# A graph-network kernel whose instruction order is written by a planner: another buffer rule, a transfer model, byte masks and other planning parameters

## The chip, the cores and the metric

The kernel runs on one core of one Trainium2 chip. Its time is the device time of one execution in microseconds (us). A core has five engines, each executing its own queue in order: TensorE (PE, matmuls and transposes), VectorE (DVE), ScalarE (ACT), GpSimd (POOL) and SyncE (SP, which here only issues transfers). They wait for each other through semaphores. Tiles lie in SBUF, 128 partitions wide; matmul results lie in PSUM, in eight banks. Everything is fp32 unless said otherwise.

## The reference

There are 32 samples of 512 nodes with 256 features. Four graph layers run in sequence; each one's result is added to its input x, which has been layer-normalised (and passed through relu) ahead of the layer. Cut to what matters:

```python
for layer in (L0, L1, L2, L3):
    x = x + layer(relu(layernorm(x)), adj)

def L0(x):                     # 4-head attention, heads of 64
    s = where(adj == 0, -inf, q @ k.T / 8)
    return softmax(s) @ v @ wo.T + bo
def gat(x, W, a, mask):        # graph attention
    h = x @ W
    e = leaky_relu(h @ a[:F] [:, None] + h @ a[F:] [None, :], 0.2)
    return elu(softmax(where(mask, e, -9e15)) @ h)
def L1(x):                     # two GATs with MLPs, the first without a mask
    o = relu(x @ mlp1_w + b1);  o = elu(gat(o, W_fc, a_fc, all)) + o
    o = relu(o @ mlp2_w + b2);  return relu(elu(gat(o, W_hand, a_hand, adj)) + o)
def L2(x): ...                 # 4-head GAT, heads of 64, masked by adj > 0
def L3(x): ...                 # 8-head GAT, heads of 32, logits plus beta * log(adj), then @ W_out
```

So every sample has eighteen 512x512 attention matrices in fp32, and no sample depends on another.

## The kernel before

**One sample.** A 512x512 matrix is kept transposed, as four tiles of 128 nodes by 512 (`p0`, `p1`, `p2`, `p3`). A tile of 128x512 f32 is called a block. All blocks come from one SBUF tag, `block`, with `BLOCKS` = 60 buffers; matmul results come from the eight PSUM banks. x is a tile of 128x4x256 with five buffers, loaded by SP, updated in place by the four layers and stored by SP; the load for a sample can start when the output of the sample five before it has left.

- `norm_t` makes statistics (DVE `stats`, `mv`), `rs` on POOL, `h` on ACT, transposes to `pt` on PE and `hT` on ACT.
- `layer0`: `qT`, `kT`, `v0`, scores `sc` on PE, exp on ACT, product with `mask0T` on DVE, additions into `total` on DVE, then `av` and the column sums `sm` on PE. `normalise` sends the sums through DRAM (`s1`, `few`, reciprocal, `s2`, `rc`) to get them on all partitions, and DVE makes `oT`; wo multiplies it. The bias is added to x by an accumulating transfer issued by POOL (`x<-boa`).
- `layer1`: mlp1 (`o1`), `first_gat` with `W_fc` (matmuls of 258 and 256 columns; row sums through the transposes of `total` and of `rs1`), mlp2 (`o3`), `second_gat` with `W_hand` (`v2`, `p2`, products with `mask1T`).
- `layer2` and `layer3` share `separable`: ACT's exp of a row broadcast `R` (eight or four transfers from DRAM by SP), then one DVE instruction for maximum and product with the mask (`mask1T`, `mask3T`). The sums over the tiles (`total`) are added by DVE for the first four heads and by accumulating transfers, issued by POOL (`p<-p`), for the last four.

**The order.** The layers do not issue instructions; they record them as `Step`s in a `Plan` (L82). `Plan.add` finds the dependencies. `Plan.order` (L169) then takes steps one by one, always the one with the smallest `(start, due)`. The start comes from a model: the engine's time, the operands' times by `cost()` (L333), release times of the samples (`STARTS`, `PACE`, `LAYERS`), and buffers. `due` comes from `PERIOD` times the sample, the length of the chain behind the step, and an offset `URGENT` for its tile's name and layer, a table of some hundred numbers. Up to four samples beyond the oldest are interleaved (`AHEAD`).

For a new tile the planner takes the buffer that comes free first by its model; it keeps some in reserve (`OWN`, `SPARE`, `KEEP`). `FILLED` = 10 blocks are withheld up to a modelled time of 190, because the preparation of masks and weights uses them:

```python
free["block"][:FILLED] = [FILLED_TO] * FILLED
...
when = max(when, sorted(free[tag])[n])
...
free[tag].remove(min(free[tag]))
```

A transfer has a length that depends on its size only, whatever else is under way. `Plan.issue` (L281) emits the steps in the order found; each engine then executes in this order, waiting where an operand or a buffer is not there. Since a helper records every step, all instructions of the four layers stand under one line in the profile, L297, and are told apart by the tiles' names.

Of the kernel before, what the change touches and what calls it, by code (L numbers as in the profile page):

```python
# [12 lines left out]
F32 = mybir.dt.float32  # L13
BF16 = mybir.dt.bfloat16
I32 = mybir.dt.int32
AF = mybir.ActivationFunctionType
# [4 lines left out]
P = 128  # L21
N = 512
NT = N // P
D = 256
# [9 lines left out]
H3, F3 = 8, 32  # L34
# [9 lines left out]

PERIOD = 107.0
STARTS, PACE = (0.0, 4.0, 19.0, 123.0), 101.0
LAYERS = (0.0, 32.0, 34.0, 184.0)

URGENT = {
    "stats:0": -231, "mv:0": -37, "rs:0": -123, "ms:0": -205, "h:0": 11, "pt:0": -750, "hT:0": 14, "mm:0": -216,  # L50
    "sc:0": -122, "p0:0": -65, "total:0": -98, "av:0": 34, "sums:0": -578, "s1:0": 49, "few:0": -6, "s2:0": 16,
    "rc:0": -235, "oT:0": 85, "mv:1": -1, "rs:1": -312, "ms:1": 79, "h:1": -294, "pt:1": -8, "hT:1": 210, "o1:1": 230,
    "sd:1": -3, "v1:1": 496, "nd:1": -243, "ew:1": 150, "p1:1": 192, "total:1": -170, "sm:1": 80, "rs1:1": -271,
    "rc:1": 295, "av:1": -43, "y:1": -155, "e:1": -181, "o2:1": 223, "o3:1": 97, "v2:1": -74, "sd2:1": 230,
    "mn:1": -599, "None:1": 532, "ew2:1": 73, "p2:1": 326, "rs2:1": -12, "u:1": 67, "x:1": 261, "stats:2": 253,
    "mv:2": -2, "ve:2": -111, "rs:2": 9, "ms:2": 327, "h:2": -217, "pt:2": 246, "hT:2": -176, "mm:2": -27,
    "vs:2": -140, "es4:2": -547, "e4:2": 121, "rd:2": -46, "R:2": 10, "p3:2": -509, "av:2": -104, "total:2": -557,
    "sm:2": 273, "r4:2": -73, "ue:2": -350, "x:2": -11, "stats:3": -7, "mv:3": -124, "ve:3": 186, "rs:3": 271,
    "ms:3": -493, "pt:3": 488, "hT:3": -507, "mm:3": -191, "vs:3": -282, "es8:3": 187, "e8:3": -10, "rT:3": -676,
    "rd:3": 450, "R:3": 367, "p3:3": -733, "av:3": -428, "total:3": 545, "sm:3": -50, "sums:3": 213, "raw:3": 11,  # L60
    "s1:3": 84, "s2:3": 121, "rc:3": -208, "oT:3": 42, "None:3": 359, "af:3": 10, "top:3": 409, "ok:3": 38,
    "values:3": -217, "rows:3": 208, "gp:3": -60, "gram:3": -190, "gab:3": 123, "sq:3": -31, "tp:3": -40,
    "res:3": 224,
}
BLOCKS, KEEP = 60, 2
KEEP_BANKS = 0
# [15 lines left out]
class Plan:  # L82
# [11 lines left out]
    OWN = dict(block=8, bank=2)  # L94
    SPARE = dict(block=2, bank=1)

    SWITCH = dict(full=0.094, columns=0.12, rows=0.2)
# [26 lines left out]
    def add(self, attribute, engine, op, args, kw):  # L124
# [8 lines left out]
        step.urgent = URGENT.get(f"{self.kinds.get(out.tensor.name)}:{step.layer}", 0.0)  # L133
        step.lasts = step.busy + lasts
        writes = [out] + ([kw["accum_out"]] if "accum_out" in kw else [])
        reads = [v for v in list(args) + list(kw.values()) if isinstance(v, bass.AP) and not any(v is w for w in writes)]
        for ap, writing in [(v, False) for v in reads] + [(v, True) for v in writes]:
            if ap.tensor.name not in self.tile_tag:
                continue
            name, box = ap.tensor.name, extent(ap)  # L140
            if name not in step.touches:
                step.touches.append(name)
            record = self.history.setdefault(name, [])
            for other, obox, owriting in record:
                bank = writing and owriting and step.engine == other.engine == "PE"
                if (writing or owriting) and other is not step and (bank or overlap(box, obox)):
                    if other not in step.before:
                        step.before.append(other)
                        other.after.append(step)
            record.append((step, box, writing))  # L150
# [6 lines left out]
    def behind(self, ap):  # L157

        self.gate = [step for step, _, writing in self.history[ap.tensor.name] if writing]

# [8 lines left out]
    def order(self):  # L169
# [16 lines left out]
        free = {tag: [0.0] * bufs for tag, (bufs, _) in self.tags.items()}  # L186
        free["block"][:FILLED] = [FILLED_TO] * FILLED
        held = {}
# [9 lines left out]
        for steps in self.samples:  # L198
            for step in steps:
                if not step.waits:  # L200
                    open_[step.engine].append(step)
        result, count, mode = [], sum(map(len, self.samples)), "full"
        oldest = 0

        def slots(step):

            when, taken = 0.0, {}
            for name in step.touches:
# [15 lines left out]
                if len(free[tag]) - n <= reserve:  # L224
                    return None
                when = max(when, sorted(free[tag])[n])
                taken[tag] = n + 1
            return when

        while len(result) < count:  # L230
            best = None
            for engine, waiting in open_.items():
                for step in waiting:
# [3 lines left out]
                    if engine == "PE" and step.mode != mode:  # L237
                        start = max(start, at[engine] + self.SWITCH[mode])
                    if best is not None and self.key(start, step) >= best[0]:
                        continue  # L240
# [7 lines left out]
            _, start, step = best  # L248
            step.start = start
            open_[step.engine].remove(step)  # L250
            at[step.engine] = start + step.busy
            if step.engine == "PE":
                mode = step.mode
            end = start + step.lasts
            for name in step.touches:
                tag, s = self.tile_tag[name], step.sample
                if name not in live:
                    live.add(name)
                    free[tag].remove(min(free[tag]))
                    held[s, tag] = held.get((s, tag), 0) + 1  # L260
                    to_come[s][tag] -= 1
                    pending[s, tag].remove(place[name])
                left[name] -= 1
                if not left[name]:
                    live.discard(name)
                    held[s, tag] -= 1
                    free[tag].append(end + self.HOP)
# [65 lines left out]
def cost(engine, op, args, kw, out):  # L333
# [15 lines left out]
    if engine == "DVE":  # L349
# [4 lines left out]
        by_pointer = op == "scalar_tensor_tensor" and isinstance(args[2], bass.AP)  # L354
        return 0.066 + 0.00105 * n + (0.06 if by_pointer else 0.0), 0.085
    if engine == "POOL":
        if op == "dma_start":
            return 1.1, (5.2 if n == N else 8.0)
        return (1.0 if n < 16 else 0.683), 0.1
    size = 4  # L360
    for _, k in (out.ap if out.tensor.name.startswith(("few", "R", "rc", "x")) else src.ap):
        size *= k
    return 0.4, 3.4 + size / 190e3


@with_exitstack
def gnn_stack_kernel(ctx: ExitStack, tc: tile.TileContext, a: dict, out: bass.AP):
# [59 lines left out]
    r3 = w3[:, :, 3 * H3 + D :]  # L427
    mask0T = const.tile([P, NT, N], BF16, name="mask0T")
    mask1T = const.tile([P, NT, N], BF16, name="mask1T")
    mask3T = const.tile([P, NT, N], F32, name="mask3T")  # L430
# [166 lines left out]
    def pipelined(stack):  # L597

        big = stack.enter_context(tc.tile_pool(name="big", bufs=1))
        psum = stack.enter_context(tc.tile_pool(name="psum", bufs=8, space=PSUM))  # L600
        dram = stack.enter_context(tc.tile_pool(name="dram", bufs=6, space=bass.MemoryType.DRAM))
        q = Plan(nc, PERIOD)
        def block(name):

            return q.tile(big, [P, N], name, BLOCKS, keep=KEEP, tag="block")

# [6 lines left out]
        def small(name, *free):  # L613
            return q.tile(big, [P, *free], name, 4)

        def half(b, t):
# [212 lines left out]
        def second_gat(o3, xt):  # L829

            v, sd = q.tile(big, [P, NT, D + 1], "v2", 2), small("sd2", NT, 2)
            for t in range(NT):
                ps = node_major(wh, t, o3, 0, D + 2)
                q.scalar.activation(v[:, t, :D], ps[:, :D], AF.Identity, bias=ones[:, 0:1])
                q.scalar.copy(sd[:, t, :], ps[:, D : D + 2])
            q.vector.memset(v[:, :, D : D + 1], 1.0)
            d = sd[:, :, 1]
# [12 lines left out]
            for t in range(0, NT, 2):  # L850
                e, u, avs, rs = block("e"), block("u"), [], small("rs2", 2, 2)
                for i in range(2):
                    av = bank("av")
                    avs.append(av)
                    for j in range(NT):
                        q.tensor.matmul(
                            av[:, : D + 1], p[j][:, col(t + i)], v[:, j, :], start=(j == 0), stop=(j == NT - 1)
                        )
# [33 lines left out]
        def separable(xt, w, nh, mask, bars):  # L892
# [12 lines left out]
            q.tensor.transpose(pt[: NT * nh, :P], es, ident)  # L905
            rT = q.tile(big, [P, P], "rT", 4, tag="turned")
            q.scalar.copy(rT[: NT * nh, :], pt[: NT * nh, :P])
            rd = q.tile(dram, [H3, N], "rd", 6)
            q.sync.dma_start(T(rd[:nh, :], "h (t p) -> t h p", p=P), rT[: NT * nh, :])
# [82 lines left out]
        def tests():  # L992
# [8 lines left out]
            for t in range(NT):  # L1001
                ai, af = q.tile(big, [P, N], "ai", BLOCKS, keep=KEEP, tag="block", dtype=I32), block("af")
                q.sync.dma_start(ai, a["adj"][t * P : (t + 1) * P, :])
# [55 lines left out]
        for i in range(B):  # L1059
# [11 lines left out]
        late = preparation(  # L1071
            lambda n: big.tile([P, N], F32, tag="block", name=n, bufs=BLOCKS),
            lambda n: psum.tile([P, N], F32, tag="bank", name=n, bufs=8),
# [424 lines left out]
```

## Time and profile before

| | before |
|---|---|
| median of 3 runs | 3901.18 us (3900.81 to 3904.83) |
| profiled execution, its own time | 3905.73 us |
| its span | 3903.9 us |
| mean granted TensorE clock | 0.995 |
| PE busy | 3824.9 us, 17400 matmuls and transposes |
| DVE busy | 3292.2 us, 7177 instructions |
| ACT busy | 2837.1 us, 6128 instructions |
| POOL busy | 519.1 us, 530 instructions |
| transfers | 292.65 MB, 1.6 thousand issues by SP and POOL in the loop over samples |

The profiled execution is 4.6 us above the median, and its span 1.8 us below its own time. A busy time is the sum of the durations that the profile gives; matmuls overlap by their pipelining, so PE's start-to-start distance is shorter than the mean of one. In the groups the DVE product with `mask3T` has a mean of 746 ns and occurs 1024 times, the DVE addition into `total` 686 ns and 808 times, ACT's exp of `R` 716 ns and 1536 times; an accumulating transfer of 256 KB lands 4.9 us after its issue.

### The profile page before, as it was taken

The numbers are of one execution on the slowest core, as the hardware profiler recorded it, in microseconds if no ns is written. First come the engines' busy times: TensorE is split into PE (matmuls) and PEld (weight loads), VectorE is DVE, ScalarE is ACT, GpSimd is POOL, SyncE is SP. The second block draws the span as 40 slices with busy tenths as digits, with TensorE's granted clock in tenths as the row PEclk, the third lists the DMA queues.
The fourth block names the chain that finished last, engine by engine and source line by source line (L and its number), as shares of the span: only waits on it lengthen the run. The fifth ranks groups of instructions, "written<-read, shape, count | busy, mean of one in ns | idle before, by whom it ended". The sixth has DMA issues, their size and how long they took to land.

```text
span 3903.9 us, 53766 instructions
## 1 busy us (share of the span) xinstructions
PE 3824.9 (98%) x17400; PEld 2230.5 (57%) x17400; DVE 3292.2 (84%) x7177; ACT 2837.1 (73%) x6128; POOL 519.1 (13%) x530
## 2 busy tenths in 40 slices
PE   8999999999999999999999999999999999999996
PEld 4555565555566555566565556565655555655643
DVE  5578988888988888988889988889888889888896
ACT  4567777777777767777677777677777777776784
POOL 0001110111110111110111111111101111101110
PEclk9999999999999999999999999999999999999998
DMA  3012331323332333332333323333323333314241
GB/s 100 19 48 61 88 93 52 92 61 82 88 84 59 93 61 82 87 76 67 82 63 89 89 66 78 81 63 88 93 58 85 70 73 88 88 55 94 46 110 48
DMA packets 217623, 292.65 MB, mean 75 GB/s; under 512 B 49915, under 2 KB 103422, under 8 KB 217334
## 3 DMA queue, kind: packets, MB, share of 16 engines
q0 software_dynamic: 68864, 111.18, 16.5%
q1 hardware_dynamic: 148196, 177.69, 14.6%
q8 instruction: 140, 2.29, 0.3%
q14 instruction: 149, 1.22, 0.1%
q10 hardware_dynamic: 274, 0.26, 0.0%
HBM read 158.79 MB, written 19.10 MB: 46 GB/s over the span
## 4 chain that ended last, share of the span: by engine, by line
PE 85%; ACT 8%; DVE 3%; issue 2%; DMA 2%; POOL 0%; SPq 0%; DVEq 0%; ACTq 0%; POOLq 0%
PE mm L297 43%; PE av L297 31%; PE pt L297 6%; ACT p L297 6%; PE sm L297 3%; DVE p L297 2%; PE sc L297 1%; DMA p<-p 1%; ACT h L297 1%; DVE total L297 1%; POOL rs L297 0%; DMA rc<-s 0%; DVE x L297 0%; DMA s<-few 0%; DVE rc L297 0%
## 5 line engine op out<-in xcount | busy, mean ns | idle before, releaser
L297 ACT ACTIVATE p<-R,e 128x512 f32<-128x512 f32 x1536 | 1001.5, 716 | 82.5 <-DVE total L297 75.6
L297 DVE SCALAR_TENSOR_TENSOR p<-p,e,mask3T 128x512 f32<-128x512 f32 x1024 | 715.0, 746 | 12.9 <-ACT p L297 12.9
L297 PE MATMUL av<-p,v 128*64 128x512 f32 (+1 forms) x2048 | 697.7, 597 | 6.6 <-ACT v L297 5.4
L297 DVE TENSOR_TENSOR total<-total,p 128x512 f32<-128x512 f32 x808 | 511.3, 686 | 0.1
L297 PE MATMUL av<-p,vs 128*32 128x512 f32 (+1 forms) x3072 | 497.9, 596 | 5.9 <-DVE p L297 5.9
L297 POOL TENSOR_TENSOR rs<-ve,mhalf 128x4 f32<-128x4 f32 x128 | 155.5, 1220 | 2367.8 <-DVE few L297 858.5
L297 POOL DMA_DIRECT2D p<-p x360 | 342.9, 1314 | 934.3 <-PE av L297 790.4
L297 PE MATMUL mm<-W_fc,o 128*128 128x256 f32 (+1 forms) x2048 | 459.5, 380 | 0.4 <-ACT o L297 0.4
L297 PEld LDWEIGHTS av<-p,v 128*64 128x64 f32 (+1 forms) x2048 | 257.6, 163 | 334.5 <-issue 278.1
L297 PEld LDWEIGHTS mm<-W_fc,o 128*128 128x128 f32 x2048 | 384.9, 190 | 83.3 <-issue 22.7
L297 DVE SCALAR_TENSOR_TENSOR p<-p,e,mask1T 128x512 f32<-128x512 f32 x512 | 352.8, 746 | 10.3 <-ACT p L297 10.1
L297 DVE TENSOR_TENSOR p<-p,mask0T 128x512 f32<-128x512 f32 x512 | 317.8, 686 | 13.9 <-ACT p L297 13.9
L297 ACT ACTIVATE h<-x,ms,rs 128x256 f32<-128x256 f32 x512 | 271.4, 593 | 69.9 <-DVE ms L297 69.8
L297 PEld LDWEIGHTS av<-p,vs 128*32 128x32 f32 (+1 forms) x3072 | 138.6, 119 | 310.0 <-issue 263.1
L297 DVE TENSOR_TENSOR total<-p,p 128x512 f32<-128x512 f32 x404 | 267.4, 690 | 39.0 <-PE av L297 22.6
L297 ACT ACTIVATE p<-sc 128x512 f32<-128x512 f32 x512 | 254.4, 673 | 3.7 <-PE sc L297 1.1
L297 PE MATMUL mm<-w,hT 128*128 128x272 f32 (+1 forms) x1024 | 253.5, 396 | 1.3 <-ACT hT L297 1.3
L297 PE MATMUL av<-v,p 128*128 128x257 f32 x1024 | 232.6, 380 | 2.7 <-ACT o L297 1.4
L297 PE MATMUL mm<-o,mlp_w 128*128 128x512 f32 x512 | 230.3, 593 | 2.1 <-DVE o L297 2.1
L297 PE MATMUL mm<-hT,mlp_w 128*128 128x512 f32 x512 | 230.9, 593 | 1.0 <-ACT hT L297 1.0
L297 PE MATMUL sc<-qT,kT 64*128 64x512 f32 x1024 | 228.9, 596 | 0.0
L297 ACT ACTIVATE e<-av,ones,rs 128x256 f32<-128x256 f32 x128 | 65.6, 562 | 220.8 <-PE av L297 108.6
(187 smaller groups left out, 5783.1 us busy)
## 6 DMA issues: line engine op xcount, KB each, us to landing
R<-rd SPq DMA_DIRECT2D x384, 256.0 KB
p<-p POOLq DMA_DIRECT2D x360, 256.0 KB, 4.9
x<-in_x_dram SPq DMA_DIRECT2D x32, 512.0 KB
x<-boa POOLq DMA_DIRECT2D x32, 512.0 KB, 6.5
rc<-s SPq DMA_DIRECT2D x128, 128.0 KB
out_dram<-x SPq DMA_DIRECT2D x32, 512.0 KB
rc<-s SPq DMA_DIRECT2D x248, 64.0 KB
s<-sums SPq DMA_DIRECT2D x94, 8.0 KB
```

The lines of the kernel that those rows point to most:

```text
L297: getattr(getattr(self.nc, attribute), op)(*args, **kw)
```

## The change

The arithmetic is the same, and so are the matmuls. Five things change.

1. The planning parameters: `PERIOD`, `STARTS`, `PACE`, `LAYERS` and the whole table `URGENT`.
2. The planner's rules. Buffers are reused in the order in which they came back (the first in the list, not the one that comes free earliest). The withheld blocks join the list when the plan passes 190. Each of SP and POOL has eight queue slots for transfers, and all transfers share one channel (`moved`), with a new function `transfer()` for their time on it; costs of transfers are changed. Steps of different engines on one PSUM bank always count as dependent.
3. `mask0T` and `mask1T` are bytes in place of bf16.
4. Blocks are 514 floats wide, of which most tiles use 512, and there are 62. `v2` of `second_gat` uses the whole width of two blocks in place of a tile of its own, so its column of ones takes two memsets in place of one.
5. The DRAM tiles have eight buffers in place of six.

```diff
-PERIOD = 107.0
-STARTS, PACE = (0.0, 4.0, 19.0, 123.0), 101.0
-LAYERS = (0.0, 32.0, 34.0, 184.0)
+PERIOD = 106.0
+STARTS, PACE = (0.0, 7.0, 20.0, 172.0), 78.0
+LAYERS = (0.0, 0.0, 120.0, 155.0)
 URGENT = {
...
-BLOCKS, KEEP = 60, 2
+BLOCKS, KEEP = 62, 2
...
+    SETUP, NOTICE, LANES = 1.4, 0.5, 8
...
-                if (writing or owriting) and other is not step and (bank or overlap(box, obox)):
+                if self.tile_tag[name] == "bank" and step.engine != other.engine:
+                    clash = True
+                else:
+                    clash = (writing or owriting) and (bank or overlap(box, obox))
+                if clash and other is not step:
...
-        free["block"][:FILLED] = [FILLED_TO] * FILLED
+        free["block"] = free["block"][FILLED:]
+        lent = FILLED
...
-                when = max(when, sorted(free[tag])[n])
+                when = max(when, free[tag][n])
...
+                    if step.transfer:
+                        start = max(start, landed[engine][0])
...
+            if lent and start >= FILLED_TO:
+                free["block"] += [FILLED_TO] * lent
+                lent = 0
...
+            if step.transfer:
+                moved = max(moved, start + self.SETUP) + step.transfer
+                end = max(end, moved + self.NOTICE)
+                landed[step.engine] = landed[step.engine][1:] + [end]
...
-                    free[tag].remove(min(free[tag]))
+                    free[tag].pop(0)
...
-        if op == "dma_start":
-            return 1.1, (5.2 if n == N else 8.0)
+        return 1.5, (5.5 if n == N else 8.0)
-    return 0.4, 3.4 + size / 190e3
+    return 0.4, (4.0 if n == N else 2.7)
+
+def transfer(op, args, kw, out):
...
+    us = pieces * (0.008 + 0.000149 * n) / min(16, out.ap[0][1])
+    if "accum_op" in kw:
+        return 2.1 * us
+    return 1.3 * us if not src.ap[0][0] else us
...
-    mask0T = const.tile([P, NT, N], BF16, name="mask0T")
-    mask1T = const.tile([P, NT, N], BF16, name="mask1T")
+    mask0T = const.tile([P, NT, N], U8, name="mask0T")
+    mask1T = const.tile([P, NT, N], U8, name="mask1T")
...
-        dram = stack.enter_context(tc.tile_pool(name="dram", bufs=6, space=bass.MemoryType.DRAM))
+        dram = stack.enter_context(tc.tile_pool(name="dram", bufs=8, space=bass.MemoryType.DRAM))
...
+        def wide(name):
+            return q.tile(big, [P, N + 2], name, BLOCKS, keep=KEEP, tag="block")
         def block(name):
-            return q.tile(big, [P, N], name, BLOCKS, keep=KEEP, tag="block")
+            return wide(name)[:, :N]
...
-            v, sd = q.tile(big, [P, NT, D + 1], "v2", 2), small("sd2", NT, 2)
+            both, sd = [wide("v2") for _ in range(2)], small("sd2", NT, 2)
+            v = [both[t // 2][:, t % 2 * (D + 1) : (t % 2 + 1) * (D + 1)] for t in range(NT)]
...
-            q.vector.memset(v[:, :, D : D + 1], 1.0)
+            for b in both:
+                q.vector.memset(T(b, "p (t c) -> p t c", t=2)[:, :, D : D + 1], 1.0)
```

## The prediction

> **What bounds it now.** I began with the page's first and fourth parts: busy shares, and the chain of work that ended last.
>
> ```profile
> PE 3824.9 (98%) x17400; PEld 2230.5 (57%) x17400; DVE 3292.2 (84%) x7177; ACT 2837.1 (73%) x6128; POOL 519.1 (13%) x530
> ...
> PE 85%; ACT 8%; DVE 3%; issue 2%; DMA 2%; POOL 0%; SPq 0%; DVEq 0%; ACTq 0%; POOLq 0%
> ```
>
> TensorE is busy for 98% of the span and carries 85% of the chain. No edit of this change touches a matmul, so its gain can only come out of what PE does not spend computing. The windows (us; busy us and instructions of PE, PEld, DVE, ACT, POOL; granted clock; DMA share; GB/s) show where that is: the ramp, a period in the middle, the end.
>
> ```profile
> 150.00:190.00 40.00, 34.73 (x133) 22.30 (x130) 16.99 (x58) 26.73 (x51) 2.03 (x2) 0.96 0.00 1
> 2068.00:2186.00 118.00, 117.58 (x540) 68.73 (x536) 102.72 (x224) 88.59 (x193) 16.94 (x17) 1.00 0.33 77
> 3750.00:3790.00 40.00, 34.43 (x173) 19.87 (x173) 38.62 (x95) 31.35 (x74) 14.43 (x14) 0.96 0.64 146
> ```
>
> In the middle PE rests 0.4 us of 118. But DVE works 102.7 of these, so only 15 us of slack stand between it and becoming the late engine: an order that lets PE run ahead of it loses. The waits of PE, asked from 415 to 3400 us, say how well the present order does:
>
> ```profile
> PE pt L297 <- ACT h L297: 10.5, 25, 0.4
> PE av L297 <- ACT v L297: 5.4, 5, 1.4
> PE mm L297 <- DVE o L297: 2.1, 1, 2.1
> ```
>
> 18.0 us in 25 samples, and no transfer among them. A timeline of PE shows the one regular wait, and what a change of matmul form costs:
>
> ```profile
> 2008.96 1.02 PE L297 MATMUL av<-p,v 128*128 128x512 f32 x2
> 2009.91 1.94 PE L297 MATMUL av<-p,vs 128*64 128x512 f32 x8
> ...
> 2057.56 0.44 PE L297 MATMUL pt<-ident,h 128*128 128x128 f32 x2 [0.42 <-ACT h L297]
> ```
>
> Two 512-column passes at 0.43 are 0.86, and the next group starts 0.95 after them: a switch between whole-array and 64-column matmuls costs 0.093 us.
>
> **How I priced the order.** Each engine executes in the order that the planner wrote. I laid both orders side by side and gave each instruction its duration in the trace of before, as start to start when back to back: DVE product 0.662, product with mask0T and addition 0.60, statistics 0.326; ACT exp 0.613, h 0.492, PSUM copies 0.05 to 0.49; PE passes 0.43 (512 columns), 0.217 (258), 0.109 (transposes). Transfers got their landings. At each PE instruction I compared two sums: PE work since an earlier place, and the ACT and DVE work that the order puts between that place and this operand. Where the second is longer, PE waits by the difference, called a shortfall here. For before this gives 0.56 per period where the trace has 0.42, and 10.6 where the ramp window loses 5.3 of 40 us and a clock of 0.96 more; so it is of the right size, within about a third.
>
> **The change, part by part.** The matmuls are the same 17400, 3695 us of passes in both. The new order has 522 switches in place of 464: 58 x 0.093 = +5.4 us.
>
> Before repeats its order every sample (114.7 us of passes, 14 switches, shortfall 0.56). The new parameters and planner make an order that repeats every four: first-GAT matmuls (W_fc) come after 134.7, 114.2, 150.8 and 59.2 us of passes (459 in all, the same), with shortfalls 1.25, 5.94, 0 and 0.24, so 7.4 against 2.2 for four samples. One place, worked out: between the transposes of rs1 and the second MLP's matmul lie 11.7 us of passes and two switches, 11.9, while the operand needs 4.2 of ACT (exps, elu) and 9.1 of DVE (7 statistics 2.3, y 1.8, o 2.4, the rest small) and 0.7 of handovers, 14.0: short by 2.1. Another: between a transposed total and layer 3's output matmul PE has 1.0 and DVE 1.8 (reciprocal, addition, oT at 0.6): short by 1.3, and by 1.1 in the three places after it.
>
> The ramp is worse. From the last w3 matmul of the third sample to a wo matmul of the sixth, PE has 95.1 of passes and 21 switches, 97.0. ACT first does 37.4 (35 exps, 21.5; the rest elu, copies and h) and then DVE 73.0 (32 mask0T products 19.3, 26 products 17.2, 35 additions 21.0, the rest 15.5), with handovers 111.3: short by 14 to 15. Likewise from the last w2 matmul of the third sample to a column sum of the fifth: 40.1 against 47.2, short by 7. Before has no such place after 420 us.
>
> Summed by stretches, before to after: two first samples 10.6 to 4.5; samples 3 to 11 5.1 to 39.2; 12 to 27 9.0 to 29.7; 28 to 31 2.7 to 7.3; tail 45.4 to 45.9. That is -6.1 + 34.1 + 20.7 + 4.6 + 0.4 = +53.7 us.
>
> Transfers: a landing of an accumulation (p<-p) is 4.9 us in the page, 3.3 alone and up to 9.5 behind others, successive ones 1.35 apart; R lands after 3.3 to 6.3, successive ones 0.7 apart. Each at its own landing they are in the sum above. Put behind one another at these spacings, before grows by 1 us, and the new order by 24: 3.4 us every four samples in front of layer 3's output matmul, six times, and 4 in the ramp. Bounds 0 and 23; I take 12, since landings between these two pictures are what the trace has.
>
> Masks as bytes: 512 products with mask0T and 640 with mask1T read a byte operand. No row has one. The nearest: the same product with a bf16 mask and an addition with an f32 second operand both take 686 ns, so the operand's type is free there. I take 0, bounds -0.05 and +0.05 us each, 36 per sample; DVE's 15 us of slack take up +1.8 outside the short places; there they lie on the path, 64 of them in the two ramp places worked out above, so -3 to +3 us.
>
> The v2 tile in two blocks: 32 more memsets of 62 ns on DVE, 2 us in all, hidden by DVE's slack in the middle (0.06 per sample on the path without it). The two more blocks, eight DRAM buffers: no instruction; what they allow is in the order. Blocks of 514 floats put buffers off their old alignment: the engines' rows show no alignment, so nothing for them, and for accumulations 0 to +0.6 us each, the spread of their quartiles; 12 per sample, in the transfers' bound.
>
> The Trainium skill, in "DMA: Bandwidth & Descriptors", section "How a descriptor splits into AXI transactions", speaks against this: a descriptor that starts off a 256-byte boundary needs one transaction more. Nine in place of eight for a 2048-byte row would make an accumulation some 0.3 us longer, an estimate; no row of before shows such a one, and PE waits for none there.
>
> Planner with first-returned blocks, queue slots, one channel, bank clashes: they are rules of planning, with no instruction; both orders were priced as they came out.
>
> Sum: 53.7 + 5.4 + 12 = +71 us. The profiled execution has 3905.73 (span 3903.9), so 3977 for a profiled one; on the median 3901.18, 3972.
>
> The clock: the ramp window lost 4% (1.6 us of 40) with PE resting 5.3. After waits of 7 and 15 us spread over 12 to 30, two or three such windows would add 3 to 5, inside the range. In the skill's "TensorE: Matmul & The Clock Gate", Part 1, an idle window of some 3.4 us halves the clock until a busy one; by it the longest single wait in the ramp, 4.8 us, could cost about 2 us more, an estimate, and none of the periodic waits of 2 us anything.
>
> **Rivals.** *The order holds better than the sums say (faster).* If ACT and DVE are never behind, only the switches are left, +5.4, and before's own losses go: starts of the samples' first GAT are 117.6 us apart, but bumps of 0.4 to 3.7 add up to 10 in 26 periods, and the ramp's 5: 3901 + 5 - 15 = 3891. For it: the new planner counts queue slots and block returns, which before's guessed. Against: the shortfalls are of durations in fixed queues, not of guesses. It decides where the shortfalls come to less than 10 us of the 54.
>
> *Bytes read slowly (slower by more).* Above 15/36 = 0.4 us per masked product DVE's slack is gone and it becomes the bound; at +0.5 us 36 x 0.5 - 15 = 3 us per sample, 96 more: 4068. No row speaks for it.
>
> *x comes late.* Only five x tiles exist, so a sample's load waits until the output five before is out (2.8 us), and takes 3.8 itself; statistics then stand at the head of DVE's queue. Before has 41 us of passes between the output and the transposes that need the statistics, the new order 15 at the closest place. The 6.6 us and four statistics (1.6) fit in 15; should the load land over 7 us late behind accumulations, it would cost 1 to 2 us in each of seven rounds of four samples, some 12: 3984.
>
> *The change does not do what it says* (an order of equal length): 3901, if shortfalls and gains cancel.
>
> **How the numbers follow.** Forecast (shortfalls are real, with or without late x) 0.84; the order holds 0.11; no change 0.04; bytes 0.01. The forecast's own range: shortfalls at 0.75 and no more bumps, 40 + 5 - 10 = +35, 3936; at 1.4 and all transfers bunched, 75 + 5 + 23 = +103, 4004. To hold 8 in 10 it reaches a little below: 3925 to 4005. A measurement of this kernel can tell about 0.2%, 8 us. Faster 0.11, same 0.04, slower 0.85.
>
> **What would show it.** Right: PE's busy share drops to 96%; windows of 40 us between 390 and 650 show PE resting 7 and 15 us, with DVE near full; the starts of first-GAT matmuls come in groups of four with 470 us between groups; the waits of PE name DVE oT, total and p, at 5 to 7 us per four samples. Wrong: those windows are full, then the order holds; a product with mask0T above 0.7 us, then bytes; long waits of PE for DMA or of DVE for x, then transfers are the price; a period of under 470 us for four samples with full PE, then before's bumps were worth more than I saw.

## The result and the profile after

The changed kernel takes 3990.5 us (median of 4 runs, 3987.6 to 3992.6) against 3901.3, a ratio of 1.0226 [1.0208, 1.0244]: 89 us slower, where 71 was forecast. Its profiled execution has 3990.61 us and a span of 3988.8, 84.9 more than before.

The page of the changed kernel: busy shares, and the accumulations.

```profile
PE 3870.7 (97%) x17400; PEld 2222.2 (56%) x17400; DVE 3264.4 (82%) x7209; ACT 2838.8 (71%) x6128; POOL 540.6 (14%) x530
...
p<-p POOLq DMA_DIRECT2D x360, 256.0 KB, 5.1
```

DVE and ACT do the same work as before (28 us less and 2 us more), and PE's busy time grew by 46 us although its matmuls are the same; part of that is a lower clock and isolated matmuls, whose ends count as busy. What PE waited for, from 415 to 3500 us (us in total, times, longest):

```profile
PE mm L316 <- DVE oT L316: 29.4, 16, 4.1
PE mm L316 <- DVE o L316: 7.7, 8, 1.3
PE mm L316 <- ACT qT L316: 6.9, 5, 1.8
PE sm L316 <- DVE total L316: 5.9, 7, 2.2
```

Before had 18 us here, mostly `h`. The prediction had named oT, total and p, and worked one place out at o; of these p is small (0.9 us), and `qT` is new. To see where the time goes I took each matmul's start and subtracted the start, the work and the switch of the matmul ahead of it, in both traces; what is left is called lost time here, "from start to start". The whole is 149 us before and 229 after: +79, and 58 switches at 0.093 make up the other 5 of the 85.

The ramp went nearly as computed: from 390 to 420 us, at a column sum, 8.8 us are lost, where the prediction had 7; from 500 to 700, at a wo matmul, 18.7, where it had 14 to 15. DVE does not rest from 619.6 us until that matmul starts at 649.7, so it is the late engine there. Four samples in the steady part take 483 to 486 us against 471 to 474, by the starts of their first-GAT matmuls: about 12.5 more, of which the prediction's sums had 6 and the transfers, if they queue, 3.4.

The chain of waits of the changed kernel in one such round, from 1690 to 1770 us, shows the largest loss (start us, us, what):

```profile
1748.76 0.96 DMA s<-few
...
1750.07 4.62 DMA rc<-s
...
1754.81 0.13 DVE oT L316
...
1755.42 0.68 DVE total L316
1756.10 1.32 DVE p L316 x2
...
1759.36 0.66 DVE p L316
1760.02 0.61 DVE oT L316
...
1760.67 9.29 PE mm L316 x34
```

The transfer rc<-s, which spreads the reciprocal row sums over the partitions, takes 4.6 us; its median in the trace is 2.2. It runs among accumulations: from 1690 to 1762 us POOL issues 24 of them, and they land after 6.2 us (median). DVE executes in order, so `oT` holds it for 5.1 us, the products and additions behind it start late, and the second `oT` releases PE at 1760.67. The timeline of PE and the windows say what follows:

```profile
1755.55 1.13 PE L316 MATMUL mm<-L_WoT,oT 128*128 128x256 f32 x4 [1.24 <-DVE oT L316]
...
1760.67 1.84 PE L316 MATMUL mm<-L_WoT,oT 128*128 128x256 f32 x4 [3.12 <-DVE oT L316]
```

```profile
650.00:656.00 6.00, 6.00 (x20) 4.81 (x21) 4.32 (x8) 4.22 (x8) 0.00 (x0) 0.58 0.01 1
...
1760.00:1765.00 5.00, 4.33 (x12) 3.53 (x13) 5.00 (x9) 2.26 (x4) 0.00 (x0) 0.66 0.12 45
```

PE rests 1.2 and 3.1 us there, and then works at half its clock: the second window's mean is 0.66, and in the trace the 256-column passes from 1760.67 start 0.427 us apart, up to 1764.4, and 0.216 after that. Nine slow passes cost some 1.7 us. The trace's clock record has five such stretches of 3.4 us, at 1276, 1761, 2246, 2730 and 3215 us, each at a wait of 2.8 to 3.1 us for the same operand, and none in before from 300 to 3600 us. After the ramp's longest wait (4.1 us at 649.7, 4.8 by start to start) the clock is 0.58 over 6 us, and 2.3 us more are lost.

### The profile page after: what moved, and what is told of

Its sections match the earlier page's. It is cut to its first block, busy times and chain, and to the rows that moved or that the text cites. A ratio compares the mean times of both kernels' runs of the same rounds, so it can differ in the third digit from the quotient of the medians.

```text
span 3988.8 us, 53702 instructions
## 1 busy us (share of the span) xinstructions
PE 3870.7 (97%) x17400; PEld 2222.2 (56%) x17400; DVE 3264.4 (82%) x7209; ACT 2838.8 (71%) x6128; POOL 540.6 (14%) x530
## 4 chain that ended last, share of the span: by engine, by line
PE 47%; DVE 5%; DMA 1%; ACT 1%; issue 1%; SPq 0%; POOL 0%; DVEq 0%; ACTq 0%
PE mm L316 22%; PE av L316 17%; PE pt L316 3%; PE sc L316 3%; DVE p L316 2%; PE sm L316 2%; DVE total L316 1%; DMA p<-p 1%; ACT p L316 0%; DVE x L316 0%; DMA R<-rd 0%; DMA rc<-s 0%; DVE o L316 0%; DVE stats L316 0%; DVE ue L316 0%
## 5 line engine op out<-in xcount | busy, mean ns | idle before, releaser
L316 PE MATMUL av<-p,vs 128*32 128x512 f32 (+1 forms) x3072 | 506.9, 598 | 3.5 <-DVE p L316 3.5
L316 POOL TENSOR_TENSOR rs<-ve,mhalf 128x4 f32<-128x4 f32 x128 | 180.2, 1409 | 2342.1 <-DVE ve L316 2190.2
L316 PE MATMUL mm<-W_fc,o 128*128 128x256 f32 (+1 forms) x2048 | 468.7, 382 | 0.3 <-DVE u L316 0.3
L316 POOL DMA_DIRECT2D p<-p x360 | 318.1, 1094 | 1019.8 <-PE av L316 561.4
L316 ACT ACTIVATE h<-x,ms,rs 128x256 f32<-128x256 f32 x512 | 280.2, 629 | 53.7 <-DVE ms L316 53.0
L316 PE MATMUL mm<-w,hT 128*128 128x264 f32 (+1 forms) x1024 | 254.4, 393 | 1.5 <-ACT hT L316 1.3
L316 PE MATMUL mm<-hT,mlp_w 128*128 128x512 f32 x512 | 243.4, 594 | 0.8 <-ACT o L316 0.8
L316 ACT COPY v<-mm 128x512 f32<-128x512 f32 (+1 forms) x256 | 118.1, 480 | 169.9 <-PE mm L316 127.2
```

Of the source, the lines that this page charges most:

```text
L316: getattr(getattr(self.nc, attribute), op)(*args, **kw)
```

## The experiments

In all of them but e7 and e8 every engine has exactly the order of the kernel that is named, so that a difference is of durations, not of the plan (e11 has one small instruction more, at its start). "Before" ran beside them at 3901.6 to 3903.7.

| run | us | against before [95%] |
|---|---|---|
| changed kernel | 3990.5 | 1.0226 [1.0208, 1.0244] |
| e1 before, bytes, blocks of 514 floats | 3924.3 | 1.0056 [1.0040, 1.0073] |
| e2 changed, short accumulations | 3939.3 | 1.0099 [1.0082, 1.0116] |
| e3 before, short accumulations | 3894.8 | 0.9984 [0.9974, 0.9993] |
| e4 changed, half of mask0T | 3979.9 | 1.0199 [1.0182, 1.0216] |
| e5 before, bytes | 3902.5 | 0.9999 [0.9989, 1.0008] |
| e6 changed, blocks aligned | 3969.6 | 1.0168 [1.0151, 1.0185] |
| e7 before, new parameters | 4184.9 | 1.0723 [1.0701, 1.0744] |
| e8 changed, planner without transfer model | 4114.6 | 1.0542 [1.0521, 1.0563] |
| e9 e1 with short accumulations | 3895.7 | 0.9983 [0.9974, 0.9993] |
| e10 e6 with short accumulations | 3940.2 | 1.0097 [1.0081, 1.0114] |
| e11 before, blocks shifted by 128 bytes | 3938.2 | 1.0093 [1.0076, 1.0110] |

**e1: the parts that are not the order.**

```diff
-    mask0T = const.tile([P, NT, N], BF16, name="mask0T")
+    mask0T = const.tile([P, NT, N], U8, name="mask0T")      # mask1T alike
-            return q.tile(big, [P, N], name, BLOCKS, keep=KEEP, tag="block")
+            return q.tile(big, [P, N + 2], name, BLOCKS, keep=KEEP, tag="block")[:, :N]
```

> The kernel before, in its own order on every engine, with both masks as bytes and all blocks 514 floats wide (60 of them, v2 in its own tile as before). If the loss of 89 us lies in the new order, as the prediction had it, this stays at the time before: 3893 to 3909 us. If byte operands or the shifted alignment of the blocks cost something, it shows here alone: 0.05 us for each of 1152 masked products would be hidden by VectorE's slack except in short places (up to 3905), 0.5 us for each would give over 3980, and accumulations that land 0.6 us later would give 3901 to 3912.

Measured 3924.3: 23 us, above what I had given either part. The masked products did not become slower (mask0T 680 ns, mask1T 745, in before 686 and 746). What moved is an accumulation, and ACT behind it. The waits of ACT from 415 to 3500 us, first of before, then of e1:

```profile
ACT v L297 <- DMA p<-p: 17.1, 25, 2.3
```

```profile
ACT v L298 <- DMA p<-p: 37.0, 26, 2.9
```

So the order before does have a place, once per sample, where an engine stands behind a transfer: an ACT copy waits for a block that an accumulation still reads. Its wait was 0.7 us with PE's work over nearly all of it, and grew to 1.4. Of PE's waits, `av` for ACT `v` went from 5.4 to 13.4 us.

DVE is a second such place: its `oT` waits for the row sums' transfer rc<-s. Whole run, first before, then e1:

```profile
L297 DVE TENSOR_TENSOR oT<-raw,rc 128x512 f32<-128x512 f32 x126 | 86.5, 688 | 20.2 <-DMA rc<-s 14.8 <-PE av L297 4.8 <-issue 0.3
```

```profile
L298 DVE TENSOR_TENSOR oT<-raw,rc 128x512 f32<-128x512 f32 x126 | 86.3, 687 | 38.9 <-DMA rc<-s 38.2 <-issue 0.3 <-DMA s<-few 0.2
```

From 415 to 3500 us this wait went from 1.4 us (once) to 21.5 (14 times), and each of PE's seven waits for `o` in e1 (5.0 us in all) comes 9 us behind one of them.

**e5: bytes alone.** The first of e1's two edits.

> The kernel before in its own order with both masks as bytes and nothing else: blocks stay 512 floats apart, so nearly all start on a 256-byte boundary. It splits the 23 us of e1. If the alignment of the blocks makes accumulations land later (5.3 us in e1's profile against 4.9), this is back at 3895 to 3909 us; if byte operands are the cost, it stays at 3917 to 3932 us.

Measured 3902.5, no difference. Bytes cost nothing that these runs can tell, and the 23 us are the blocks' new places.

**e11: alignment alone.** Pitch, width and masks as before, and every block, with the other tiles of its pool, 128 bytes further on. That the blocks of before start on 256-byte boundaries is taken from the layout; no trace shows an address.

```diff
+        pad = stack.enter_context(tc.tile_pool(name="pad", bufs=1)).tile([P, 32], F32, name="pad")
+        nc.vector.memset(pad, 0.0)
         big = stack.enter_context(tc.tile_pool(name="big", bufs=1))
```

> The kernel before in its own order, with bf16 masks and blocks of 512 floats as before, but a tile of 128 bytes lies ahead of the blocks, so that all of them start 128 bytes past a 256-byte boundary (one more memset of that tile at the start). If the start of a row against a 256-byte boundary is what made accumulations slower in e1, where 7 of 8 blocks were off, this loses as much or a little more: 3920 to 3932 us, successive landings of accumulations about 1.5 us apart against 1.43. If it is the distance of 2080 bytes between blocks, or their width, it is back at 3896 to 3908 us.

Measured 3938.2: 36 us, more than I had expected, with all blocks off the boundary in place of (by the layout) seven of eight. So neither the pitch nor the width is needed for the loss. Accumulations issued within 1 us of each other land 1.43 us apart (median) in before, 1.49 in e1, 1.52 here; the median landing went from 4.9 to 5.3 and 5.4 us. The waits of ACT and of PE from 415 to 3500 us:

```profile
ACT v L297 <- DMA p<-p: 39.7, 26, 2.9
```

```profile
PE av L297 <- ACT v L297: 16.8, 26, 2.3
PE mm L297 <- DVE o L297: 10.9, 14, 1.7
```

Both places are later still than in e1: DVE's `oT` waits 49.7 us for rc<-s in the whole run.

```profile
L297 DVE TENSOR_TENSOR oT<-raw,rc 128x512 f32<-128x512 f32 x126 | 86.5, 689 | 54.1 <-DMA rc<-s 49.7 <-issue 3.6 <-PE av L297 0.5
```

Are the plain transfers slower too, whose tiles moved with the rest? By the traces from 415 to 3500 us, no: R, written into the same blocks, lands after 4.1 us (median) in before, 4.2 in e1 and 4.1 here, rc<-s after 2.2, 2.1 and 2.1. This leaves what they stand behind as the cause of the late ones, which e9 tests.

**e9: e1 with short accumulations.** The edit is made where the steps are issued; e2, e3 and e10 have it too.

```diff
                 for attribute, op, args, kw in step.calls:
+                    if "accum_op" in kw and kw["out"].ap[-1][1] == N:
+                        kw = dict(kw, out=kw["out"][:, :64], in_=kw["in_"][:, :64])
```

> e1 (the order before, bytes, blocks 514 floats apart) with each accumulation p<-p cut to 64 of 512 columns (the rest of these sums is left out). If the alignment costs 23 us because the accumulations land later, this falls to where e3 was, 3891 to 3900 us. If another transfer or an engine suffers from the alignment, some 15 us or more stay: 3908 to 3922 us.

Measured 3895.7, the same as e3 (3894.8). With short accumulations nothing of the 23 us is left, and DVE's wait for rc<-s is back to 0.7 us. Together with the unchanged landings of R and rc<-s: the alignment acts through the accumulations. Short ones do not show it at all: their successive landings are 0.88 us apart with the blocks on the boundary (e3) and off it (e9).

**e2 and e3: short accumulations in both orders.**

> The changed kernel in its own order, but each of the 360 accumulating transfers p<-p moves 64 of its 512 columns (the rest of these sums is left out). Theory A, transfers: in the new order the accumulations of two samples come in bursts, exps that need their blocks and the row sums rc come late behind them, and this is some 50 of the 89 us: 3930 to 3945 us. Theory B, engines: PE waits because VectorE and ScalarE have too much ahead of an operand, and a transfer's lateness only names waits that would be there anyway: not under 3978 us.

> The kernel before with the same cut: each accumulation p<-p moves 64 of 512 columns (the rest of these sums is left out). Both theories: its order has other work under every transfer (no wait of PE for one from 415 to 3400 us), so 3890 to 3901 us. A gain of over 20 us would mean that both kernels pay for transfers, and the comparison with the changed kernel would have to be made against this.

Measured 3939.3 and 3894.8. The new order gives back 51 us, the old one 7. Theory B, that a transfer's lateness only names waits that would be there anyway, falls. In e2 the round of four samples is 475.5 us long, the second `oT` of the chain above makes no wait, and PE's waits for oT from 415 to 3500 us are down to a third:

```profile
PE mm L318 <- DVE oT L318: 10.2, 6, 4.1
PE mm L318 <- DVE o L318: 9.2, 10, 1.3
```

**e6 and e10: the new order with aligned blocks.**

```diff
-            return q.tile(big, [P, N + 2], name, BLOCKS, keep=KEEP, tag="block")
+            return q.tile(big, [P, N], name, BLOCKS, keep=KEEP, tag="block")
-            both, sd = [wide("v2") for _ in range(2)], small("sd2", NT, 2)
+            both, sd = [q.adopt(big.tile([P, N + 2], F32, tag="v2", name="v2", bufs=4), "v2", BLOCKS, KEEP, "block")
+                        for _ in range(2)], small("sd2", NT, 2)
```

> The changed kernel in its own order on every engine, with blocks of 512 floats, aligned as before, and v2 in four wide buffers of its own. If alignment costs in any order what it cost in e1 or more (exps and row sums stand behind the accumulations in the new order), 3950 to 3970 us. If it costs only where an order has short cover, as the one before has for these landings, and the new order's bursts hide a longer landing in a queue, 3980 to 3992 us. What is left above 3901 is the order's own price.

> e6 (the changed kernel in its own order, blocks aligned) with each accumulation p<-p cut to 64 of 512 columns (the rest of these sums is left out). What is left over the kernel before is the part of the new order that no accumulation makes: shortfalls and switches, by the prediction 54 + 5 at most. With the alignment acting through the accumulations alone it equals e2, 3934 to 3942 us; if alignment also acts elsewhere, 3920 to 3930 us.

Measured 3969.6 and 3940.2. The alignment costs 21 us in the new order too, and PE's wait for `qT` (6.9 us) is gone with it. Some 5 of the 21 go with the clock: e6's trace has two of the half-clock stretches of 3.4 us in the rounds, where the changed kernel has five. With short accumulations the alignment makes no difference (3940.2 and 3939.3), as in e9.

What is left in e10 is a matter of the engines. In its trace the chain of work that ended last has 114 us of DVE from 760 to 3500 us, where e3's has 11, and only 6 us of transfers; PE's waits in its rounds name DVE's o and oT. ACT waits 62 us for R from 415 to 3500 us, where before has no such wait, but little of this is on the chain.

**e4: less work for VectorE.**

```diff
                 for attribute, op, args, kw in step.calls:
+                    if op == "tensor_tensor" and args[2].tensor.name.startswith("mask0T"):
+                        args = tuple(v[:, : N // 2] for v in args)
```

> The changed kernel in its own order, but the 512 products with mask0T cover 256 of 512 columns (half of that mask is left out), which takes about 0.27 us each off VectorE, 4.3 us per sample. Theory A: only the two places of the ramp with 32 such products each have VectorE as the late engine; their 7 and 14 us shrink by up to 8.6 each, the periodic waits stay: 3970 to 3980 us. Theory B, VectorE late in every round of four samples: 16 products in each of two or three short places, 3930 to 3955 us.

Measured 3979.9: 10.6 us less than the changed kernel, out of 135 us of DVE work taken away (512 products at 419 ns in place of 683). From start to start, 300 to 760 us lose 27.4 in place of 33.3, and a round of four samples takes 484.6 us as before the edit: the rounds do not turn on these products, as theory A had it. In the ramp only some 6 came back, where I had allowed for 7 and 8.6. The next cause seems close behind: there `oT` now waits for rc<-s (0.4 and 0.35 us), and PE's longest wait is 4.6 us where it was 4.1.

**e7 and e8: is it the parameters or the planner?** e7 is before with the new `PERIOD`, `STARTS`, `PACE`, `LAYERS` and `URGENT`. e8 is the changed kernel without these lines of the planner:

```diff
-                    if step.transfer:
-                        start = max(start, landed[engine][0])
...
-            if step.transfer:
-                moved = max(moved, start + self.SETUP) + step.transfer
-                end = max(end, moved + self.NOTICE)
-                landed[step.engine] = landed[step.engine][1:] + [end]
```

> The kernel before with the new planning parameters alone (its own planner, aligned blocks, bf16 masks). Priced in the way of the prediction, with transfers behind one another at 1.37 and 0.7 us: shortfalls of 368 us with the start and the tail against 90 for before, 98 more switches, so 281 us above before: 4182 us, between 4130 and 4240. If only the parameters made the loss and the planner's new rules gave some of it back or nothing, it lies above the changed kernel; if the planner's new rules made the loss, it lies between 3890 and 3960.

> The changed kernel with the planner's queue slots and its single transfer channel taken out, all else as changed. Priced in the same way, 124 us above the changed kernel: 4114 us, between 4060 and 4160. If the transfer model in the planner is what makes its order poor, it is below 3990 us instead.

Measured 4184.9 and 4114.6, within 3 us of both forecasts. (For e7 the terms written there, 278 and 98 switches at 0.093, add to 287 and not 281: 4188.) The new parameters alone cost 281 us, and the planner's new rules, with the rest of the change, bring most of that back; the transfer model alone is worth 124 us with these parameters. What the new rules do with the old parameters was not run, so how the loss divides between the two stays open; the new pair made a poorer order than the old pair had. These two also test the way of pricing an order on two orders that were not known when it was made. They test it in sum: e8's price is a difference from the measured time, and e7's could be near by the same kind of offset as below.

No run beat the kernel before, except e3 and e9, whose short accumulations leave out part of the sums.

## Why the prediction was right, and where its terms were not

The mechanism was right: a new order in which DVE, ACT and transfers come behind at places that the old one covered. The sum of 71 came near the order's share (45 + 20 = 65) by terms that were off in both directions, and one term, worth 21, was missing; that the total lies within 18 us is partly luck.

| term | predicted | measured | from |
|---|---|---|---|
| shortfalls and switches | 53.7 + 5.4 = 59 | 45 | e10 - e3 |
| accumulations bunched in the new order | 12, between 0 and 23 | 20 | (e6 - before) - (e10 - e3) |
| alignment of the blocks | 0, or in the transfers' bound | 21 | changed - e6 |
| bytes | 0 | 0 | e5 |
| all | 71 | 86 | 89 in the runs of the changed kernel; before's median moves by 2 us between sets of runs |

**Shortfalls** were too large by 14, about the factor of 0.75 that set the range's low end. The large places are near to what was computed: in the round of 1481 to 1966 us, 1.38 us lost for 1.3 at the first matmul of layer 3's output, 1.36 for 2.1 at the second MLP; the ramp as above. (The terms given for the 1.3, 1.8 of DVE against 1.0 of PE, make 0.8.) By stretches, from start to start, e10 loses 5 us less than e3 up to 300 us, 24 more from 300 to 760, 26 more up to 3500 and 7 less after that; with the switches this is the 45. The prediction had -6 for the first two samples, +59 from the third to the last, and nothing for the tail. So about half of the difference is a tail that no sum had right, and the rest lies in the samples between. How the small places went, one by one, I did not follow. The accumulations of e10 and e3 still take 0.88 us each, so a part of the 45 may be theirs.

**Transfers.** Of the bounds 0 and 23 the upper one, with transfers behind one another, was the better: 20 measured, some of it the lower clock after the waits, and e7 and e8, priced in this way, were near.

**Alignment** is the step that failed. The prediction gave accumulations up to 0.6 us each, which covers what they took (0.3 to 0.5 more in the median), and left it in a bound with the reason that PE waits for none of them in before. (It called 0.6 the spread of the landings' quartiles; these are 4.6 and 6.2 us, a spread of 1.6.) That asked the wrong engine: PE waited for no transfer, but ACT waited for one in every sample, 17.1 us in all, its cover was nearly used up, and DVE's for rc<-s was not much better. Before had the sign in its own chain, where these are among the longest pieces:

```profile
570.26 6.35 DMA p<-p
...
1395.65 6.23 DMA p<-p
...
1873.78 6.71 DMA rc<-s
...
2694.23 6.11 DMA p<-p
...
3165.68 6.65 DMA p<-p
```

Each lies in one of the five samples between 500 and 3300 us whose first-GAT starts are more than 118.5 us apart (118.6 to 121.3; the others 117.6 to 118.0). These are the bumps that the prediction counted without a cause; in e3 every such distance is 117.6 or 117.7. The rule of the Trainium skill that spoke against the change ("DMA: Bandwidth & Descriptors", "How a descriptor splits into AXI transactions") was cited and set aside. By that page the first transaction of a descriptor that is not aligned starts at the boundary below; for 2048 bytes this makes nine of eight, though not every length gets one more. e11 agrees in kind for rows of 2048 bytes, since there only the tiles' start was moved; rows of 256 bytes (e9 against e3) show no difference. In size, successive landings went 6% further apart (1.43 to 1.52), where one transaction in eight more would be 12% of the moving part, an estimate; the estimate of 0.3 us for a landing lies beside 0.4 in e1 (4.9 to 5.3), 0.5 in e11 and 0.3 between e6 and the changed kernel (4.9 to 5.1), which hold queueing as well.

**The clock.** The estimate of about 2 us after the ramp's longest wait, from "TensorE: Matmul & The Clock Gate", Part 1, was met: 2.3 us. But waits of 2.8 to 3.1 us in the rounds also cost some 1.7 us each, five times, where I had read the rule as excluding the periodic ones; the waits were longer than the 2 us that I had for them. Not every such wait costs it: in e6 those at 1753 and 2236 us are followed by half clock, the one of 3.1 us at 1271 is not.

**Rivals.** The order did not hold. Bytes are free. x came late twice in the steady part, 10.6 us of DVE's waits in all, and no wait of PE names it. Of what was to be seen, PE's busy share fell to 97%, not 96%, and PE's busy time from 390 to 420 us is 26.8, so it seems to rest 3.2 us where 8.8 are lost: a matmul that stands alone counts as busy to its modelled end, and the losses show only from start to start.

## What to carry to other kernels

Where one engine is full and every engine executes a fixed order, a new order can be priced before it runs: work between two places on the full engine against the work that the other queues put between them, with transfers one behind the other and not each at its best. Ask the waits of every engine for transfers, not only those of the bottleneck: an engine whose wait is just covered is where a slightly slower transfer comes out. When a tile gets a few elements more, look at where the next ones start; here 8 bytes per row cost as much as a third of the reordering.

## What the runs showed of the hardware that I had not expected

- Moving the blocks, and the tiles behind them, by 128 bytes cost 36 us of 3902. Successive landings of the 360 accumulating transfers of 256 KB went from 1.43 to 1.52 us apart, while the plain transfers R into the same blocks landed as before (4.1 us, median), and accumulations with rows of 256 bytes stayed 0.88 apart (e3, e9).
- A masked product or maximum-and-product of 128x512 takes the same time with a byte operand as with bf16 (683 and 686 ns, 746 and 746), the other operands being f32.
- An accumulation of 64 columns still lands after 2.8 us, successive ones 0.88 apart (e2); one of 512 columns after 5.1, 1.48 apart, in the same order and place (the changed kernel): eight times the bytes for 1.7 times the spacing.
